# A planned attention block on one core: first rows loaded ahead of the large operands, and three small steps given a choice of two engines

## The chip, the core and the metric

The kernel runs on one core of one Trainium2 chip. The metric is the device time of one execution in microseconds (us); lower is better. The five engines are called as the profile calls them: PE (matmul; PEld is its weight load), DVE, ACT, POOL and SP. Each engine works through its own instruction stream in order, and an instruction that waits for a semaphore holds up all that stands behind it in that stream. SP only issues DMAs here.

## What is computed

The reference is a transformer block with modulation, for 2 sequences of 2048 tokens of 256 features, all in f32. Cut to what matters:

```
mod = silu(c) @ wmod                       # 6 rows of 256 per sequence: sa, ca, ga, sb, cb, gb
ga, gb = sign * max(|.|, 0.25)
h = layernorm(x) * (1 + ca) + sa
x = x + ga * attention(h)                  # 2 query heads, 1 key/value head of 128, rotary, causal
h = layernorm(x) * (1 + cb) + sb
x = x + gb * experts(h)                    # 8 experts, 256 -> 1024 -> 256, gate with a threshold
```

## The kernel before, in words

There are two stages. `experts` (from some 507 us to the end) is a loop over items of 256 tokens for each of 8 experts. Its code isn't touched. `attention` (up to some 502 us) is touched, and it isn't a loop: it is a list of small steps, each a Python function that issues a few instructions, put into an order by a planner.

**The planner.** `Plan.add` notes a step: an engine, an estimated cost in us, the steps it comes after, the buffers it takes and gives back (`room`: 6 PSUM tiles `ps`, 9 row tiles `x`, 3 `xn`, and so on), a rank, and an extra delay `late` for what a DMA takes to land. `Plan.run` plays these costs through in an event loop: whenever an engine is free, the open step with the lowest rank that is ready and finds its buffers is put on it. When all are placed, the steps are issued in the order in which they began. So the estimated costs decide the order in every engine's stream, and nothing else does; on the chip each stream then runs at its own real durations. A step can't overtake another in its stream, even when it is ready and the other isn't.

**The loads (lines 271 to 294 and 435 to 439).** `load` plans a DMA on SP at a cost of 0.06 + KB/180 us. The first ones have the rank `first` (-100) and so go in the order of the code: `c_sb` (2 KB), `wm_0` (512 KB: the weights of the first modulation), `wqkv_sb` (512 KB), the first quarter of the rotary table (512 KB). `wm_1` (1024 KB) and `wo_sb` (256 KB) have rank 0.5. A tile's own rows of x (128 KB, `load_x`) have the tile's rank.

**The modulation.** `by_feature` (L322) multiplies `wm_0` with silu(c) on PE; `by_feature_out` (L330) leaves `modT`, shift and scale by feature. For each sequence b, `gates` (L345) and `rows` (L373) are two PE steps that need `wm_1`; `gates_out` (L354 to L368, 8 instructions on DVE, scheduled as one step) makes `woG` and `gb_bc`, and `rows_out` (L380, L381) `mod_bc`. Their rank is 0.6 + 2b.

**A tile (128 tokens, `tile_steps`).** The tiles have ranks 0, 1, 2 and so on: four of sequence 0, four of sequence 1, and so on; 32 in all. The first part of a tile is what the change touches:

- load rows; mean and variance on DVE (L412, L414); 1/sqrt on POOL (L418, L419)
- `xn` (L444, DVE): rows less mean, times 1/sqrt
- `turn` (L453, PE): two transposes into PSUM, one for each half of the features
- `hT(0)` (L461, ACT) and `hT(1)` (L463, DVE): scale and shift of the two halves, PSUM to SBUF
- `qkv` (L472, PE), 128 x 512; the copy of v (L478, ACT)
- rotary: two products (L488, and L496 in two instructions), then their sum (L505), all on DVE
- `turn_rot` (L512, PE), copies of k and q (L515, L517, ACT)

Then come scores (L528, L532), row maximum (L539, L546, DVE), exponentials (L555, ACT), transposes (L601), weighted values (L611), projection (L645), residual (L652), the second layernorm (L667, L670, with 1/sqrt on POOL again), the layout copy `halves` on POOL (L677), and the gate's logits (L692, L701). After each group of tiles the gate is worked out, and POOL issues one indirect DMA for each tile into the first expert's list (L808), each after the one before it. Work of the first expert on two items (L950, L967) has rank 1000 and fills PE at the end of the stage. The loads of the first two experts' weights wait for all modulation steps, since they take the space of `wm_0`, `wm_1`, `wo_sb` and `sc_bc`.

Of the kernel before, what the change touches and what calls it, by code (L numbers as in the profile page):

```python
# [18 lines left out]
ALU = mybir.AluOpType  # L19
AX = mybir.AxisListType  # L20

P = 128
B, T, D = 2, 2048, 256
# [19 lines left out]
class Plan:  # L43
# [2 lines left out]

    def __init__(self, room):
        self.room = dict(room)  # L50
        self.steps = []

    def add(self, eng, cost, do, after=(), take=(), give=(), rank=0.0, late=0.0):


        self.steps.append((eng, cost, do, tuple(after), tuple(take), tuple(give), rank, late))
        return len(self.steps) - 1

    def run(self):
        LINK = 0.12  # L60
        need = [len(s[3]) for s in self.steps]
        then = [[] for _ in self.steps]
        for n, s in enumerate(self.steps):
            for m in s[3]:
                then[m].append(n)
        queues = {}
        ready = [0.0] * len(self.steps)
        open_ = {n for n, c in enumerate(need) if c == 0}
        free, ends, order, now = {}, [], [], 0.0
        while open_ or ends:  # L70
            for n in sorted(open_, key=lambda n: (self.steps[n][6], n)):
                eng, cost, do, _, take, give, _, late = self.steps[n]
                if free.get(eng, 0.0) > now or ready[n] > now:
                    continue
                if any(self.room[r] < take.count(r) for r in take):
                    continue
                for r in take:
                    self.room[r] -= 1
                free[eng] = now + cost
                ends.append((now + cost + late, n))  # L80
                open_.discard(n)
                order.append(n)
            times = [e for e, _ in ends] + [f for f in free.values() if f > now]
            times += [ready[n] for n in open_ if ready[n] > now]
            now = min(t for t in times if t > now)
            for e, n in [x for x in ends if x[0] <= now]:
                ends.remove((e, n))
                for r in self.steps[n][5]:
                    self.room[r] += 1
                for m in then[n]:  # L90
                    need[m] -= 1
                    ready[m] = max(ready[m], e + LINK)
                    if need[m] == 0:
                        open_.add(m)
        assert len(order) == len(self.steps)
        for n in order:
            self.steps[n][2]()
        return now


# [92 lines left out]
def attention(  # L193
# [5 lines left out]
    nc = tc.nc  # L199
# [17 lines left out]
        return small.tile(shape, dtype, tag=tag, name=f"{tag}{u}")  # L217

    plan = Plan(room)
    first = -100.0  # L220


# [13 lines left out]
    wqkv_sb = const.tile([P, KD, 4 * HS], F32, name="wqkv_sb")  # L236
# [33 lines left out]

    def load(dst, src, kb, rank=first, **how):
        return plan.add(
            "SP", 0.06 + kb / 180.0, lambda: nc.sync.dma_start(dst, src), late=2.0, rank=rank, **how
        )


    l_c = load(c_sb, cT.rearrange("(k p) b -> p k b", p=P), 2)
    l_x0 = None
    wm = wmod.rearrange("(k p) f -> p k f", p=P)
    l_m0 = load(wm_0, wm[:, :, : 2 * D], 512)  # L280
    l_qkv = load(wqkv_sb, wqkvT.rearrange("(k p) f -> p k f", p=P), 512)
    l_rope = [
        load(rope_sb[:, ds(4 * q, 4)], rope.rearrange("(q n p) (z f) -> p q n z f", p=P, n=4, z=2)[:, q],
             512, rank=first if q == 0 else q * 8 - 7.5)
# [2 lines left out]

    sheet_of_0 = lists[0].rearrange("(p c) f -> p c f", p=P)
    load(sheet_of_0[:, : AHEAD * CI, :], kept.front, 8, rank=0.7)
    l_m1 = load(wm_1, wm[:, :, 2 * D :], 1024, rank=0.5)  # L290
    l_wo = load(wo_sb, woT.rearrange("(h p) d -> p h d", p=P), 256, rank=0.5)
    l_wg = load(wgt_sb, wgt.rearrange("(k p) e -> p k e", p=P), 9, rank=0.5)
    l_bg = load(bgt_sb, bgt.partition_broadcast(P), 5, rank=0.5)
    l_b1 = load(b1_sb, b1T, 32, rank=6.0)
# [5 lines left out]
    def load_expert(e):  # L300
        w1_e = wpool.tile([P, KD, FF], F32, tag=f"w1_{e}", name=f"w1_{e}")
        nc.sync.dma_start(w1_e, w1[e].rearrange("(k p) f -> p k f", p=P))
        w2_e = wpool.tile([P, NF, D], F32, tag=f"w2_{e}", name=f"w2_{e}")
        nc.sync.dma_start(w2_e, w2[e].rearrange("(f p) d -> p f d", p=P))
        weights.append((w1_e, w2_e))
# [8 lines left out]
        after=[s_sc], rank=first,  # L314
# [24 lines left out]
    for b in range(B):  # L339

        def gates(b=b):
            box["pg", b] = pg = ps_tile(f"pg{b}")
            for g, which in enumerate((2, 5)):
                for k in range(KD):
                    nc.tensor.matmul(  # L345
                        pg[:, ts(g, D)], sc_bc[:, k, b, :], wm_1[:, k, ts(which - 2, D)],
                        start=(k == 0), stop=(k == KD - 1),
                    )

        def gates_out(b=b):  # L350

            u = f"_g{b}"
            g_sb = work([P, 2 * D], "g_sb", u)
            nc.vector.tensor_copy(g_sb, box["pg", b])  # L354
            sign = work([P, 2 * D], "sign", u)
            nc.vector.tensor_scalar(sign, g_sb, 0.0, 2.0, ALU.is_ge, ALU.mult)
            size = work([P, 2 * D], "size", u)
            nc.vector.scalar_tensor_tensor(size, g_sb, -1.0, g_sb, ALU.mult, ALU.max)
            nc.vector.tensor_scalar(size, size, 0.25, None, ALU.max)
            ga = work([P, D], "ga", u)  # L360
            nc.vector.scalar_tensor_tensor(
                ga, sign[:, :D], 1.0, size[:, :D], ALU.subtract, ALU.mult
            )
            nc.vector.scalar_tensor_tensor(
                gb_bc[:, b, :], sign[:, D:], 1.0, size[:, D:], ALU.subtract, ALU.mult
            )
            for h in range(NH):
                nc.vector.tensor_tensor(woG[:, b, h, :], wo_sb[:, h, :], ga, ALU.mult)  # L368

        def rows(b=b):  # L370
            box["pr", b] = pr = ps_tile(f"pm2{b}")
            for k in range(KD):
                nc.tensor.matmul(  # L373
                    pr, sc_bc[:, k, b, :], wm_1[:, k, D : 3 * D],
                    start=(k == 0), stop=(k == KD - 1),
                )

        def rows_out(b=b):
            pr = box["pr", b]
            nc.vector.tensor_copy(mod_bc[:, b, :D], pr[:, :D])  # L380
            nc.vector.tensor_scalar(mod_bc[:, b, D:], pr[:, D:], 1.0, None, ALU.add)  # L381

        r = 0.6 + 2 * b
        g = plan.add("PE", 1.8, gates, after=[s_bc, l_m1], take=["ps"], rank=r)
        m_wo.append(plan.add("DVE", 4.0, gates_out, after=[g, l_wo], give=["ps"], rank=r))
        g = plan.add("PE", 1.8, rows, after=[s_bc, l_m1], take=["ps"], rank=r)
        m_mod.append(plan.add("DVE", 0.9, rows_out, after=[g], give=["ps"], rank=r))

    prev, l_first = [], []
    for e in range(RES):  # L390
        prev = [
            plan.add(
                "SP", 11.0, lambda e=e: load_expert(e), after=m_wo + m_mod + [m_T] + prev, late=2.0,
                rank=8.0 + 4 * e,
            )
        ]
        l_first += prev
# [26 lines left out]
    def tile_steps(b, i, r, group, g):  # L424
# [7 lines left out]
        def add(eng, cost, do, after=(), **how):  # L432
            return plan.add(eng, cost, do, after=after, rank=r, **how)
# [2 lines left out]
            st["x"] = work([P, D], "x", u)  # L436
            nc.sync.dma_start(st["x"], x[b, ts(i, P), :])

        n_x = add("SP", 0.8, load_x, late=2.0, take=["x"])
        n_n = moments("a" + u, st, [n_x], add)  # L440

        def xn():
            st["xn"] = work([P, D], "xn", u)
            nc.vector.tensor_scalar(  # L444
                st["xn"], st["x"], st["mv"][:, 0:1], st["rstd"], ALU.subtract, ALU.mult
            )

        n_n = add("DVE", 0.42, xn, [n_n], take=["xn"])

        def turn():  # L450
            st["pt"] = ps_tile(f"pt{u}")
            for k in range(KD):
                nc.tensor.transpose(st["pt"][:, ts(k, P)], st["xn"][:, ts(k, P)], ident)  # L453

        def hT(k):
            if "hT" not in st:
                st["hT"] = work([P, KD, P], "hT", u)
            scale_k, shift_k = modT[:, KD + k, b : b + 1], modT[:, k, b : b + 1]
            src, dst = st["pt"][:, ts(k, P)], st["hT"][:, k, :]
            if k == 0:  # L460
                nc.scalar.activation(dst, src, AF.Identity, bias=shift_k, scale=scale_k)  # L461
            else:
                nc.vector.tensor_scalar(dst, src, scale_k, shift_k, ALU.mult, ALU.add)  # L463

        n_t = add("PE", 0.32, turn, [n_n], take=["ps"], give=["xn"])
        n_0 = add("ACT", 0.27, lambda: hT(0), [n_t, m_T], take=["hT"])
        n_1 = add("DVE", 0.29, lambda: hT(1), [n_t, m_T, n_0], give=["ps"])

        def qkv():
            st["pq"] = ps_tile(f"pq{u}")  # L470
# [11 lines left out]
        def rot(z):  # L482
# [18 lines left out]
        n_r0 = add("DVE", 0.6, lambda: rot(0), [n_q, l_rope[i // 4]], take=["big"])  # L501
        n_r1 = add("DVE", 0.75, lambda: rot(1), [n_q, n_v, n_r0], give=["ps"])
        n_r = add(
            "DVE", 0.55,
            lambda: nc.vector.tensor_tensor(st["t", 0], st["t", 0], st["t", 1], ALU.add),  # L505
            [n_r0, n_r1],
        )

# [916 lines left out]
```

## Time and profile before

| what | value |
|---|---|
| median of 3 runs | 1676.8 us (1675.76 to 1677.0) |
| the profiled execution | 1677.0 us, of which its span 1675.2 us |
| PE busy over the span | 1622.3 us (97%) |
| DVE / ACT / POOL busy | 677.0 (40%) / 576.4 (34%) / 855.0 us (51%) |
| mean granted clock of PE | 0.988 |

The span is what the trace covers; 1.8 us of the execution lie outside it. A share of busy time is a mean over the two stages: in the attention stage POOL is nearly idle and DVE is nearly full at first, in the experts' stage it is the other way round. Tables by stretch of time show this, and the prediction reads such a table. PE's busy time counts a slow matmul as busy, so its clock has to be looked at beside it.

### The profile page before, as it was taken

What the parts mean: (1) busy time and instruction counts of PE and PEld (TensorE: products, weight loads), DVE (VectorE), ACT (ScalarE), POOL (GpSimd) and SP (SyncE); (2) the same over time, 40 slices, a digit from 0 to 9 for tenths busy, and PEclk for the clock granted to TensorE, in tenths of its full rate; (3) what the DMA queues carried; (4) which work ended last, traced back from release to release, by engine and by line L of the source; (5) the groups of instructions that cost most, each with busy time, mean ns of one, the idle gap of its engine ahead of it and who ended that gap; (6) DMA issues with size and microseconds to landing.
All of it is one profiled execution on the core that took longest, in us unless ns stands there. A gap on an engine that the chain in (4) does not pass through costs nothing.

```text
span 1675.2 us, 26699 instructions
## 1 busy us (share of the span) xinstructions
PE 1622.3 (97%) x7666; PEld 1352.3 (81%) x7666; DVE 677.0 (40%) x2220; ACT 576.4 (34%) x1390; POOL 855.0 (51%) x991
## 2 busy tenths in 40 slices
PE   6999999999998998999999999999999999999996
PEld 3667677676787887888888888888888888888886
DVE  5987767666642222322333222222322222222322
ACT  2555555555632222222222222222222232222222
POOL 2332222021117777756775775676677477734443
PEclk9999999999998998999999999999999999999998
DMA  6211000000024334335334433533533333433332
GB/s 218 101 39 32 26 29 29 17 13 17 13 50 101 57 63 109 58 58 108 58 60 101 78 57 61 106 59 62 109 60 61 63 58 57 67 59 57 63 57 47
DMA packets 166045, 106.36 MB, mean 63 GB/s; under 512 B 111136, under 2 KB 157344, under 8 KB 165856
## 3 DMA queue, kind: packets, MB, share of 16 engines
q0 software_dynamic: 42064, 46.84, 17.8%
q1 hardware_dynamic: 116048, 46.22, 11.7%
q10 hardware_dynamic: 7872, 12.58, 2.4%
q8 instruction: 26, 0.43, 0.1%
q14 instruction: 35, 0.29, 0.1%
HBM read 50.39 MB, written 31.87 MB: 49 GB/s over the span
## 4 chain that ended last, share of the span: by engine, by line
PE 61%; DMA 3%; issue 3%; POOL 3%; POOLq 1%; DVE 0%; SPq 0%; DVEq 0%
PE h L1145 31%; PE y L1136 30%; POOL out L1288 2%; DMA xp<-xr 1%; DMA xr<-feats,at 1%; POOL list L1278 0%; POOL xr L1257 0%; DMA out<-yo,who 0%; POOLq L1038 0%; POOL out L1320 0%; POOL at L1299 0%; POOLq L1086 0%; POOLq L1299 0%; DVE yo L1235 0%; POOL to L1270 0%
## 5 line engine op out<-in xcount | busy, mean ns | idle before, releaser
L1145 PE MATMUL h<-xT,w 128*128 128x256 f32 (+1 forms) x2752 | 660.6, 373 | 16.3 <-DVE xT L1199 8.9
L1136 PE MATMUL y<-w,g 128*128 128x256 f32 x2640 | 654.3, 379 | 0.0
L1171 ACT ACTIVATE g<-h,b_sb 128x256 f32<-128x256 f32 (+1 forms) x688 | 320.4, 466 | 847.8 <-PE h L1145 845.7
L1145 PEld LDWEIGHTS h<-xT,w 128*128 128x128 f32 x2752 | 514.7, 191 | 86.6 <-DVE xT L1199 10.5
L1136 PEld LDWEIGHTS y<-w,g 128*128 128x128 f32 x2640 | 498.8, 190 | 66.3
L1288 POOL DMA_INDIRECT out<-yo,who x173 | 283.2, 1637 | 215.1 <-DVE yo L1235 163.0
L1199 DVE COPY xT<-xp 128x512 uint16<-128x512 uint16 x172 | 68.0, 437 | 630.4 <-PE h L1145 608.0
L1278 POOL DMA_INDIRECT list<-new,to x228 | 233.7, 1025 | 99.3 <-POOL new L1273 46.7
L1257 POOL DMA_INDIRECT xr<-feats,at x172 | 173.8, 1010 | 100.9 <-POOL at L1299 70.2
L611 PE MATMUL pav<-pT,v 128*128 128x256 f32 x544 | 144.0, 387 | 0.6 <-ACT pT L605 0.5
L528 PE MATMUL psc<-kT,qT 128*128 128x512 f32 (+3 forms) x320 | 142.9, 532 | 0.3 <-DVE s L539 0.2
L539 DVE TENSOR_SCALAR_CACHE_REDUCE s<-psc 128x512 f32<-128x512 f32 (+3 forms) x160 | 96.2, 605 | 68.3 <-PE psc L528 46.0
L555 ACT ACTIVATE s<-s,nmx 128x512 f32<-128x512 f32 (+3 forms) x160 | 103.9, 651 | 46.5 <-DVE nmx L546 46.2
L611 PEld LDWEIGHTS pav<-pT,v 128*128 128x128 f32 x544 | 96.1, 192 | 29.1 <-issue 19.6
L1223 DVE TENSOR_TENSOR yb<-y,b_bc 128x256 f32<-128x256 f32 x165 | 62.6, 419 | 135.9 <-PE y L1136 135.8
L418 POOL TENSOR_SCALAR rstdf<-mvf 128x1 f32<-128x1 f32 x32 | 8.3, 260 | 195.2 <-DVE mvf L414 115.4
L605 ACT COPY pT<-ptr 128x512 f32<-128x512 f32 (+1 forms) x144 | 77.2, 563 | 52.3 <-PE pav L611 30.4
L601 PE MATMUL ptr<-ident,s 128*128 128x128 f32 x544 | 76.4, 280 | 2.7 <-ACT s L555 2.7
L601 PEld LDWEIGHTS ptr<-ident,s 128*128 128x128 f32 x544 | 65.6, 145 | 16.6 <-ACT s L555 5.0
L1214 DVE SCALAR_TENSOR_TENSOR gate<-gb_bc,mcur,part 128x256 f32<-128x256 f32 x172 | 75.8, 482 | 3.0
L808 POOL DMA_INDIRECT list<-entry,place x32 | 33.7, 1054 | 76.9 <-DVE place L805 56.6
L528 PEld LDWEIGHTS psc<-kT,qT 128*128 128x128 f32 x320 | 57.5, 190 | 14.0 <-issue 6.3
(157 smaller groups left out, 1069.7 us busy)
## 6 DMA issues: line engine op xcount, KB each, us to landing
w<-in_w ACTq DMA_DIRECT2D x12, 1024.0 KB, 7.8
x<-in_x SPq DMA_DIRECT2D x32, 128.0 KB, 2.1
out<-x SPq DMA_DIRECT2D x32, 128.0 KB, 1.7
w<-in_w SPq DMA_DIRECT2D x4, 1024.0 KB, 9.1
feats<-hp SPq DMA_DIRECT2D x32, 128.0 KB, 1.7
list<-new,to POOLq DMA_INDIRECT x228
out<-yo,who POOLq DMA_INDIRECT x173
xr<-feats,at POOLq DMA_INDIRECT x172, 2.8
```

What stands on the lines that cost most here:

```text
L528: nc.tensor.matmul(ps[:, :w], st["qT"][:, h, :], kT[:, ds(c * SC, w)], start=True, stop=not last)
L539: nc.vector.tensor_scalar(s[:, :w], st["sc", h, c][:, :w], 1.0, None, ALU.mult, ALU.max, accum_out=st["mx", h][:, c : c + 1],)
L555: nc.scalar.activation(s[:, :w], s[:, :w], AF.Exp, bias=st["nmx", h], accum_out=st["den"][:, h, c : c + 1],)
L601: nc.tensor.transpose(ptr[:, j, h, :], s[:, ds((c0 + j) * P % SC, P)], ident)
L605: nc.scalar.copy(pT[:, :m], st["ptr", c0][:, :m])
L611: nc.tensor.matmul(st["pav"][:, : NH * P], v[:, c0 + j, :], st["pT", c0][:, j].rearrange("p h t -> p (h t)"), start=(c0 + j == 0), stop=(c ...
L1136: last = pe.matmul(ys[c], gs[f % 4][:, ts(c, P)], weights[e][1][:, f, :], start=(f == 0), stop=(f == NF - 1),)
L1145: last = pe.matmul(hs[f % 4][:, :w], weights[e][0][:, k, ts(f, P)], xT[:, k, :w], start=(k == 0), stop=(k == KD - 1),)
L1171: act.activation(gs[f % 4][:, :w], hs[f % 4][:, :w], AF.Gelu_apprx_tanh, bias=b1_sb[:, at : at + 1],).then_inc(sem["act"], 1)
L1257: pool.indirect_dma_start(out=xr[:, ts(c, 2 * D)], out_offset=None, in_=feats, in_offset=bass.IndirectOffsetOnAxis(ap=at[:, c : c + 1], ax ...
L1278: pool.indirect_dma_start(out=lists[e], out_offset=bass.IndirectOffsetOnAxis(ap=to[:, j : j + 1], axis=0), in_=new[:, j, :], in_offset=Non ...
L1288: pool.indirect_dma_start(out=rows, out_offset=bass.IndirectOffsetOnAxis(ap=who[:, c : c + 1], axis=0), in_=yo[:, c, :], in_offset=None, b ...
```

## The change

- `Plan.add` takes a list of engines with a cost for each. `Plan.run` places such a step on the first engine of the list that is free when the step is ready, and hands the engine to the step's function. Which engine it is, is fixed when the program is built; the chip doesn't choose.
- Three steps of each tile get such a list: `xn` (DVE 0.42 or POOL 0.65), `hT(1)` (DVE 0.41 or ACT 0.46), and the rotary sum L505 (DVE 0.58 or POOL 1.0).
- The costs of loads become max(0.5, KB/360); a tile's rows cost 0.5 instead of 0.8, an expert's weights 6.0 instead of 11.0.
- Ranks of loads: `c_sb` first, then the rows of tiles 0 and 1, then `wm_0` and `wqkv_sb`, then the first quarter of the rotary table and the rows of tiles 2 and 3, then `wm_1` and `wo_sb`.
- The rank of the steps of `gates` and `rows` becomes 1.6 + 3b instead of 0.6 + 2b.

```diff
     def add(self, eng, cost, do, after=(), take=(), give=(), rank=0.0, late=0.0):
+        if isinstance(eng, str):
+            eng, cost, do = [eng], [cost], lambda _, do=do: do()
...
-                eng, cost, do, _, take, give, _, late = self.steps[n]
-                if free.get(eng, 0.0) > now or ready[n] > now:
+                engs, costs, do, _, take, give, _, late = self.steps[n]
+                idle = [(e, c) for e, c in zip(engs, costs) if free.get(e, 0.0) <= now]
+                if not idle or ready[n] > now:
                     continue
+                eng, cost = idle[0]
...
-            "SP", 0.06 + kb / 180.0, lambda: nc.sync.dma_start(dst, src), late=2.0, rank=rank, **how
+            "SP", max(0.5, kb / 360.0), lambda: nc.sync.dma_start(dst, src), late=2.0, rank=rank,
...
-    l_c = load(c_sb, cT.rearrange("(k p) b -> p k b", p=P), 2)
+    l_c = load(c_sb, cT.rearrange("(k p) b -> p k b", p=P), 2, rank=first - 3)
-    l_m0 = load(wm_0, wm[:, :, : 2 * D], 512)
-    l_qkv = load(wqkv_sb, wqkvT.rearrange("(k p) f -> p k f", p=P), 512)
+    l_m0 = load(wm_0, wm[:, :, : 2 * D], 512, rank=first - 1)
+    l_qkv = load(wqkv_sb, wqkvT.rearrange("(k p) f -> p k f", p=P), 512, rank=first - 1)
-    l_m1 = load(wm_1, wm[:, :, 2 * D :], 1024, rank=0.5)
-    l_wo = load(wo_sb, woT.rearrange("(h p) d -> p h d", p=P), 256, rank=0.5)
+    l_m1 = load(wm_1, wm[:, :, 2 * D :], 1024, rank=first + 1)
+    l_wo = load(wo_sb, woT.rearrange("(h p) d -> p h d", p=P), 256, rank=first + 1)
...
-        r = 0.6 + 2 * b
+        r = 1.6 + 3 * b
...
-                "SP", 11.0, lambda e=e: load_expert(e), after=m_wo + m_mod + [m_T] + prev, late=2.0,
+                "SP", 6.0, lambda e=e: load_expert(e), after=m_wo + m_mod + [m_T] + prev, late=2.0,
...
-        n_x = add("SP", 0.8, load_x, late=2.0, take=["x"])
+        early = {0.0: -2, 1.0: -2, 2.0: 0, 3.0: 0}
+        n_x = plan.add(
+            "SP", 0.5, load_x, late=2.0, take=["x"], rank=first + early[r] if r in early else r
+        )
...
-        n_n = add("DVE", 0.42, xn, [n_n], take=["xn"])
+        n_n = add(["DVE", "POOL"], [0.42, 0.65], xn, [n_n], take=["xn"])
...
-            if k == 0:
+            if eng == "ACT":
                 nc.scalar.activation(dst, src, AF.Identity, bias=shift_k, scale=scale_k)
             else:
                 nc.vector.tensor_scalar(dst, src, scale_k, shift_k, ALU.mult, ALU.add)
...
-        n_1 = add("DVE", 0.29, lambda: hT(1), [n_t, m_T, n_0], give=["ps"])
+        n_1 = add(
+            ["DVE", "ACT"], [0.41, 0.46], lambda eng: hT(1, eng), [n_t, m_T, n_0], give=["ps"]
+        )
...
         n_r = add(
-            "DVE", 0.55,
-            lambda: nc.vector.tensor_tensor(st["t", 0], st["t", 0], st["t", 1], ALU.add),
+            ["DVE", "POOL"], [0.58, 1.0],
+            lambda eng: of[eng].tensor_tensor(st["t", 0], st["t", 0], st["t", 1], ALU.add),
             [n_r0, n_r1],
         )
```

`of` is the table from "DVE" and "POOL" to the engine's instruction issuer.

More of the change, by code (lines that the diff above doesn't have):

```diff
@@ L81, in run @@
                 open_.discard(n)
-                order.append(n)
+                order.append((n, eng))
             times = [e for e, _ in ends] + [f for f in free.values() if f > now]
@@ L95, in run @@
         assert len(order) == len(self.steps)
-        for n in order:
-            self.steps[n][2]()
+        for n, eng in order:
+            self.steps[n][2](eng)
         return now
@@ L219, in attention @@
     plan = Plan(room)
+    of = {"DVE": nc.vector, "POOL": nc.gpsimd}
     first = -100.0
@@ L272, in load @@
         return plan.add(
-            "SP", 0.06 + kb / 180.0, lambda: nc.sync.dma_start(dst, src), late=2.0, rank=rank, **how
-        )
-    l_c = load(c_sb, cT.rearrange("(k p) b -> p k b", p=P), 2)
-    l_x0 = None
+            "SP", max(0.5, kb / 360.0), lambda: nc.sync.dma_start(dst, src), late=2.0, rank=rank,
+            **how
+        )
+    l_c = load(c_sb, cT.rearrange("(k p) b -> p k b", p=P), 2, rank=first - 3)
     wm = wmod.rearrange("(k p) f -> p k f", p=P)
-    l_m0 = load(wm_0, wm[:, :, : 2 * D], 512)
-    l_qkv = load(wqkv_sb, wqkvT.rearrange("(k p) f -> p k f", p=P), 512)
+    l_m0 = load(wm_0, wm[:, :, : 2 * D], 512, rank=first - 1)
+    l_qkv = load(wqkv_sb, wqkvT.rearrange("(k p) f -> p k f", p=P), 512, rank=first - 1)
     l_rope = [
@@ L437, in load_x, with xn @@
             nc.sync.dma_start(st["x"], x[b, ts(i, P), :])
-        n_x = add("SP", 0.8, load_x, late=2.0, take=["x"])
+        early = {0.0: -2, 1.0: -2, 2.0: 0, 3.0: 0}
+        n_x = plan.add(
+            "SP", 0.5, load_x, late=2.0, take=["x"], rank=first + early[r] if r in early else r
+        )
         n_n = moments("a" + u, st, [n_x], add)
-        def xn():
+        def xn(eng):
             st["xn"] = work([P, D], "xn", u)
-            nc.vector.tensor_scalar(
+            of[eng].tensor_scalar(
                 st["xn"], st["x"], st["mv"][:, 0:1], st["rstd"], ALU.subtract, ALU.mult
             )
-        n_n = add("DVE", 0.42, xn, [n_n], take=["xn"])
+        n_n = add(["DVE", "POOL"], [0.42, 0.65], xn, [n_n], take=["xn"])
         def turn():
@@ L453, in turn, with hT @@
                 nc.tensor.transpose(st["pt"][:, ts(k, P)], st["xn"][:, ts(k, P)], ident)
-        def hT(k):
+        def hT(k, eng):
             if "hT" not in st:
@@ L465, in tile_steps @@
         n_t = add("PE", 0.32, turn, [n_n], take=["ps"], give=["xn"])
-        n_0 = add("ACT", 0.27, lambda: hT(0), [n_t, m_T], take=["hT"])
-        n_1 = add("DVE", 0.29, lambda: hT(1), [n_t, m_T, n_0], give=["ps"])
+        n_0 = add("ACT", 0.27, lambda: hT(0, "ACT"), [n_t, m_T], take=["hT"])
+        n_1 = add(
+            ["DVE", "ACT"], [0.41, 0.46], lambda eng: hT(1, eng), [n_t, m_T, n_0], give=["ps"]
+        )
         def qkv():
```

## The prediction, made before the changed kernel was built

> **What bounds the kernel.** The page gives PE 97% of the span, so only time in which PE is idle or slow can be won. I read the stretches of time first. Columns: stretch, length, busy time of PE, PEld, DVE, ACT and POOL with instruction counts, granted PE clock, DMA share, GB/s.
>
> ```profile
> 0.00:10.00 10.00, 3.54 (x16) 3.49 (x16) 2.67 (x7) 1.49 (x2) 3.99 (x19) 1.00 0.80 243
> 10.00:20.00 10.00, 5.57 (x13) 2.48 (x14) 2.75 (x8) 1.24 (x4) 0.82 (x2) 1.00 0.96 300
> 20.00:30.00 10.00, 9.05 (x36) 5.63 (x34) 8.48 (x28) 2.94 (x8) 1.59 (x4) 1.00 0.23 78
> 30.00:40.00 10.00, 6.54 (x18) 3.22 (x18) 8.01 (x26) 1.82 (x5) 3.05 (x7) 0.83 0.67 221
> 40.00:60.00 20.00, 19.33 (x96) 12.97 (x97) 18.26 (x74) 12.60 (x39) 4.07 (x10) 1.00 0.43 153
> 60.00:80.00 20.00, 19.05 (x96) 13.39 (x95) 17.81 (x61) 7.89 (x27) 8.30 (x18) 1.00 0.25 80
> ...
> 200.00:250.00 50.00, 50.00 (x242) 36.02 (x241) 31.23 (x113) 27.25 (x73) 10.10 (x20) 1.00 0.08 24
> ```
>
> PE is idle for 15.3 us of the first 40 (10 less each of 3.54, 5.57, 9.05, 6.54), for 5.6 us from 40 to 200, and hardly after that. From 40 to 100 DVE is 90% busy: there it is the second bound. Next, who kept PE waiting before 40 us, and how fast its matmuls ran (waits: total, times, longest; timeline: start, length):
>
> ```profile
> PE pm L322 <- DMA wm<-in_wmod: 6.0, 1, 6.0
> PE pt L453 <- DVE xn L444: 5.2, 3, 2.4
> PE pr L512 <- DVE t L505: 2.1, 1, 2.1
> ...
> 13.05 3.78 PE L472 MATMUL pq<-wqkv_sb,hT 128*128 128x512 f32 x4 [0.55 <-ACT hT L461]
> ...
> 43.50 1.88 PE L472 MATMUL pq<-wqkv_sb,hT 128*128 128x512 f32 x4
> ...
> 8.71 5.70 SPq L437 DMA_DIRECT2D x<-in_x x5
> ...
> 26.08 0.42 DVE L412 BATCH_NORM_STATS2 sta<-x 128x6 f32<-128x256 f32 x1
> ```
>
> The same four matmuls take 3.78 us at 13.05 and 1.88 at 43.50: PE is slow until it has been busy for a while. The next two such groups take 2.93 and 2.36 us. Slowness therefore costs 1.9 + 1.05 + 0.5 = 3.4 us, and the first 40 us lose 15.3 + 3.4 = **18.7 us**. Tile 1's rows are issued only after the large loads (8.71), and its statistics stand at 26.08, behind a block of modulation work on DVE: PE runs one tile alone, and waits along its chain.
>
> At the stage's end PE finishes at 499.46 and the experts begin at 506.86. That tail hangs on PE's last result, so what PE gains earlier moves everything after it. The experts' code and data are the same: 0.
>
> **Part 1, the loads.** SP issues one DMA each 0.5 us. `wm_0` moves from 1.26 to about 2.27, behind two row loads, with 256 KB ahead of it. It landed 4.6 us after issue; I let it land at 6.9 (5.9 before), **+1.0**. Rows of tiles 0 and 1, 2.1 us from issue to landing where nothing is in front, are there at 3.4 and 3.9 (tile 0 before: 2.78 + 6.3 = 9.1). `wm_1` landed at 4.06 + 9.1 = 13.2 with 3.2 MB sent up to it; now it is 3.1 MB, so it stays. DVE is through with its constants and `sc_bc` at about 5.5; statistics (0.6), POOL (0.24 + 0.58) and `xn` (0.41) put tile 0's `xn` at some 7.4, under `by_feature`. So PE does `by_feature` 6.9 to 10.45 (3.54 as before), then transposes of two tiles; `modT` (0.23), `hT(0)` and `hT(1)` (0.46 and 0.41) lead to `qkv` at 11.9 instead of 13.05. Lost so far: 6.9 waiting, 0.7 around `hT`, 1.9 for a cold first `qkv`: 9.5. The Trainium skill (TensorE: Matmul & The Clock Gate, Part 1) says the clock is released after some 3.4 us of sustained work; by that rule `by_feature` might warm PE and save the 1.9, but in the row `qkv` ran slow right after it, with 3.6 us between. I take the row.
>
> **Part 2, the order up to 40 us.** After the first `qkv`, the second tile's `qkv` (rows here long ago) is work for the 2.07 us in which PE waited for L505, and tiles 2 and 3 (rows landing at about 10) for the waits at exponentials and at `xn` (2.37). `gates` of sequence 1 at rank 4.6 instead of 2.6 puts its DVE block (8 instructions, 0.69 + 0.43 + 0.69 + 0.43 + 0.43 + 0.42 + 0.75 = 3.8 us) behind tiles 1 to 4, not ahead of their `xn`. What was lost after the first `qkv` is 18.7 - 6.0 - 2.3 - 0.5 - 1.9 = 8.0 us. The new loss there, s, lies between 0 (all covered) and 8.0 (the block of sequence 0 still stands in DVE's stream, and PE waits behind it). I take s = 3.5, a little under half: two more tiles are ready, but one DVE block remains. Gain: 18.7 - 9.5 - 3.5 = **5.7 us** (1.2 to 9.2). The loads of the experts' weights, which wait for the modulation, come some us later; they landed about 9.1 us after issues at 33 to 37, and are first read near 470, so nothing waits.
>
> **Part 3, the choice of engines.** A step leaves DVE when DVE is busy in the plan. A tile costs DVE at most `xn` 0.40, `hT(1)` 0.40 and the sum 0.55 = 1.35 us less. Of PE's idle from 40 to 200, those named for the sum are 2.2 and for `xn` 0.2 us; clearing them while part comes back as another wait gives **2 us** (range -3 to 5: five is most of the 5.6, the loss is that of rival C in a mild form). After 200 PE waits 0.2 us for the sum in all: 0 (-1 to 3). ACT is half busy (27 of 50 us) and takes `hT(1)` in the same 0.46 us as its first half: 0.
>
> Price of the sum on POOL: no row has it. Low end: `halves` moves 512 elements in 0.61, so 384 take some 0.5 us. High end: The Trainium skill (GPSIMD Engine Reference, §3.1 and §4.1) sends elementwise work to VectorE and gives 2.6 cycles of 1.2 GHz an element with two inputs, estimate 384 x 2.17 ns = 0.83, with the 0.24 of POOL's smallest row about 1.05 us against 0.55 on DVE. I take 1.0, as the two inputs make the rule nearer. By the rule alone some 20 moved sums lengthen their tiles' chains by 0.45 x 20 = 9 us, **against** the change; by the row DVE's stream was 90% full, and a sum that queues there waits as long. PE works on other tiles meanwhile, so I charge nothing. The skill's SBUF — State Buffer (SBUF: two separate sides) adds that POOL and a DVE instruction with two SBUF inputs shut each other out. L670 is such a one: of 32, the median is 0.484 and the longest 0.696, so a collision was worth at most 0.2 us here. With POOL's new 0.6 + 1.0 us a tile, 32 of them are 6 us of DVE at the very worst, and hidden after 200.
>
> **Sum.** 5.7 + 2.0 + 0 = 7.7 us. From the profiled execution, 1677.0, it leaves 1669.3; that execution lies 0.2 above the median, so 1669.1.
>
> **Rivals.** About 0.2% (3.4 us) is what can be told from no change: 1673.4 and 1680.2.
> A, the forecast, 1669.1 (1662 to 1673.4): 0.55.
> B, the start is gained and the engines' choice brings nothing, 1676.8 - 5.7 = 1671.1: 0.10. Against it stand the waits for L505.
> C, slower: POOL's stream. Its indirect DMA to the list takes 1.05 us and it waited up to 2.4 us for the one before, 17.5 us in all; a moved `xn` or sum behind it comes late, and `turn` or `turn_rot` holds up PE's whole stream. 40 moved steps at 0.5 us are 20 us: 1676.8 - 7.7 + 20 = 1689. It decides from 22 such delays on (11 us of loss against 7.7 of gain, past 1680.2). Against it: POOL is busy for 10 of 50 us, and its 64 square roots went through the same stream. 0.22.
> D, same: s = 8, PE stalls again behind DVE's modulation block, gain 1.2: 1675.6. 0.13.
>
> Faster 0.65, same 0.13, slower 0.22. The least time is a start with s = 0 and nearly all of the 7.3 us lost from 40 to 200 (5.6 idle, and 1.7 by a granted clock of 0.83 in the stretch from 120 to 130): 16 us, 1661. To leave out no more than 2 in 10 the range goes some way into C: **1661 to 1684**; the forecast's own is 1662 to 1673.4.
>
> **What would show it.** In the changed profile: first `qkv` near 11.9; PE idle from 0 to 40 near 11 us, not 15.3, most of it before 7; statistics of tiles 1 to 3 before 13 us; PE idle from 40 to 200 near 3.5 us; the experts' first matmul near 499. C would show PE waiting for POOL at L453 and L512; D a wait of PE for L444 or L505 after 17 us. Wrong outright: PE gaps after 200, where there were none, from an order that the new costs made.

## The result: 1658.1 us, and the profile after

| | before | changed |
|---|---|---|
| median of 5 runs | 1676.8 us (1675.76 to 1678.69) | 1658.1 us (1657.47 to 1661.85) |
| ratio, 95% interval | | 0.9892 (0.9879 to 0.9906): 1.1% faster |
| profiled execution / its span | 1677.0 / 1675.2 us | 1661.85 / 1660.0 us |
| experts' first matmul | 506.86 us | 490.42 us |

18.7 us were gained where 7.7 were forecast. The attention stage ends 16.4 us earlier in the profiles; where the other 2.3 us come from isn't known. The five executions of the changed kernel differ by up to 4.4 us, and the profiled one was the longest. Stretches of time of the changed kernel (columns as in the prediction), then PE's waits up to 40 us and from 40 to 200:

```profile
0.00:10.00 10.00, 3.30 (x16) 3.33 (x17) 4.02 (x10) 1.49 (x2) 5.87 (x23) 1.00 0.74 243
10.00:20.00 10.00, 9.88 (x29) 5.53 (x29) 6.57 (x19) 2.32 (x7) 3.82 (x6) 1.00 1.06 354
20.00:30.00 10.00, 9.74 (x47) 6.24 (x46) 8.01 (x33) 7.22 (x22) 4.04 (x5) 1.00 0.25 80
30.00:40.00 10.00, 10.00 (x49) 6.70 (x48) 9.05 (x32) 4.24 (x15) 7.47 (x13) 1.00 0.23 69
40.00:60.00 20.00, 19.21 (x97) 13.79 (x96) 17.84 (x60) 10.31 (x33) 10.42 (x20) 1.00 0.71 248
60.00:80.00 20.00, 20.00 (x104) 13.87 (x103) 18.60 (x76) 12.34 (x37) 10.26 (x16) 1.00 0.21 67
...
PE pm L329 <- DMA wm<-in_wmod: 6.7, 1, 6.7
...
PE pr L525 <- POOL t L518: 2.2, 2, 1.5
PE pt L464 <- POOL xn L455: 1.3, 1, 1.3
PE ph L705 <- DVE hx L683: 0.2, 1, 0.2
```

After its first operand has landed (6.7 us, forecast 6.9) PE isn't named as waiting once up to 40 us. DVE is busy for 27.7 of these 40 us (21.9 before), and POOL for 21.2 (9.5 before). The moved steps, over the stage (count, busy, mean ns):

```profile
L455 POOL TENSOR_SCALAR xn<-x,mva,rstda 128x256 f32<-128x256 f32 x23 | 29.1, 1267 | 20.1 <-PE pt L464 18.9
L518 POOL TENSOR_TENSOR t<-t,t 128x384 f32<-128x384 f32 x23 | 23.0, 999 | 33.1 <-DVE before L764 8.1 <-DVE t L509 7.4 <-DVE ge L786 7.2
L472 ACT ACTIVATE hT<-pt,modT 128x128 f32<-128x128 f32 x58 | 23.7, 459 | 19.6 <-PE pt L464 19.6
```

23 of 32 `xn`, 23 of 32 sums and 26 of 32 `hT(1)` (58 less the 32 of `hT(0)`) left DVE.

**Where the 16.4 us come from.** PE's last matmul of the stage went from 499.46 to 482.19. PE's idle time before it: 15.3 to 7.1 us up to 40, 5.6 to 3.7 from 40 to 200, 3.1 to 2.8 after, together 10.3. The rest of that time PE was busy, 475.5 us before and 468.6 now with the same matmuls: 6.9 us less by slow matmuls alone. Most of it stands in the column of the granted clock. Rows of the kernel before, then of the changed one:

```profile
120.00:130.00 10.00, 9.15 (x41) 6.96 (x42) 7.67 (x30) 4.27 (x11) 3.44 (x6) 0.83 0.09 28
450.00:460.00 10.00, 7.88 (x35) 5.90 (x34) 7.16 (x23) 5.89 (x18) 3.89 (x5) 0.87 0.05 15
460.00:470.00 10.00, 10.00 (x58) 8.98 (x57) 4.88 (x28) 4.07 (x9) 3.12 (x5) 0.96 0.27 67
...
120.00:130.00 10.00, 10.00 (x57) 7.94 (x55) 5.22 (x24) 5.86 (x18) 4.94 (x6) 1.00 0.05 14
450.00:460.00 10.00, 10.00 (x49) 8.40 (x48) 5.41 (x21) 4.64 (x9) 3.93 (x5) 1.00 0.29 70
460.00:470.00 10.00, 10.00 (x52) 8.78 (x51) 3.93 (x24) 5.65 (x11) 1.66 (x3) 1.00 0.05 16
```

The kernel before lost 1.7 us of clock three times: from 30 to 40 us (10 us at 0.83), from 120 to 130, and from 450 to 470. That is 5.1 of the 6.9 us, and the changed kernel's rows have 1.00 in these places. The slow first `qkv` doesn't show in this column: the row from 10 to 20 has 1.00 in both kernels. The tail up to the experts' first matmul grew from 7.4 to 8.2.

### The profile page after: what moved, and what is told of

Same layout as the page of the kernel before. It is cut to its first block, busy times and chain, and to the rows that moved or that the text cites. A ratio compares the mean times of both kernels' runs of the same rounds, so it can differ in the third digit from the quotient of the medians.

```text
span 1660.0 us, 26742 instructions
## 1 busy us (share of the span) xinstructions
PE 1613.9 (97%) x7666; PEld 1347.2 (81%) x7666; DVE 659.0 (40%) x2148; ACT 584.4 (35%) x1416; POOL 904.5 (54%) x1037
## 4 chain that ended last, share of the span: by engine, by line
PE 61%; DMA 3%; POOL 3%; issue 3%; POOLq 1%; DVE 0%; DVEq 0%; SPq 0%
PE h L1158 31%; PE y L1149 31%; DMA xp<-xr 2%; POOL out L1301 2%; DMA xr<-feats,at 1%; POOL list L1291 1%; POOL xr L1270 0%; DMA out<-yo,who 0%; DMA sign_p_next<-g_sb_r_next 0%; DMA g_sb_r_next<-feats,next_at 0%; POOLq L1051 0%; POOL out L1333 0%; POOL at L1312 0%; POOLq L1099 0%; POOLq L1312 0%
## 5 line engine op out<-in xcount | busy, mean ns | idle before, releaser
L614 PE MATMUL ptr<-ident,s 128*128 128x128 f32 x544 | 72.6, 274 | 2.1 <-ACT s L568 1.9
L1312 POOL COPY at<-sheet 128x2 int32 x85 | 62.9, 740 | 14.5 <-DMA xp<-xr 13.5
```

The costliest lines, as they stand in the source:

```text
L614: nc.tensor.transpose(ptr[:, j, h, :], s[:, ds((c0 + j) * P % SC, P)], ident)
```

## The experiments

The mark in all of them is the experts' first matmul. A second profile of the changed kernel (b1) had it at 489.3 instead of 490.4, so a difference of 1 us says nothing. Total times serve less: beside six of the runs (a1 to a4, e1, e2) the kernel before itself took some 1700 us, and in the profiles of these six the experts' stage is 17 to 36 us longer than in the first profile of the kernel before. Each row of the table is one profiled execution; `delay` is the planner's assumed delay between engines, otherwise 0.12 us. `idle` is PE's before its last matmul of the stage, `slow` its busy time over 468.6 us, `tail` the gap to the mark; with 468.6 us they add up to the mark.

| kernel | mark | idle to 40 / to 200 / after | slow | tail |
|---|---|---|---|---|
| before | 506.9 | 15.3 / 5.6 / 3.1 | 6.9 | 7.4 |
| d2 before, delay 0.13 | 507.9 | 14.3 / 7.0 / 2.9 | 7.0 | 8.2 |
| d4 before, delay 0.11 | 512.0 | 15.6 / 4.6 / 5.8 | 9.4 | 8.1 |
| c4 before, new step costs | 514.4 | 15.3 / 5.3 / 5.0 | 10.7 | 9.6 |
| d1 loads alone | 501.5 | 10.0 / 6.0 / 2.4 | 6.3 | 8.3 |
| a1 loads and step costs, no choice | 507.7 | 10.4 / 6.7 / 5.0 | 7.5 | 9.6 |
| e1 choice alone | 505.3 | 15.7 / 4.2 / 2.6 | 5.9 | 8.3 |
| a2 choice and step costs | 506.8 | 15.2 / 3.1 / 6.7 | 5.0 | 8.2 |
| c1 choice and load costs | 499.4 | 12.7 / 1.4 / 3.1 | 5.4 | 8.2 |
| b2 changed, old load costs | 500.8 | 12.0 / 2.3 / 4.6 | 4.8 | 8.6 |
| a3 changed, rows by rank | 490.1 | 8.5 / 1.5 / 2.1 | 1.1 | 8.3 |
| a4 changed, old modulation rank | 494.0 | 8.5 / 3.7 / 2.7 | 2.0 | 8.6 |
| b3 changed, `xn` on DVE | 490.3 | 7.6 / 1.3 / 3.4 | 0.7 | 8.7 |
| b4 changed, sum on DVE | 496.1 | 7.7 / 3.5 / 3.4 | 3.3 | 9.6 |
| c3 changed, `hT(1)` on DVE | 494.7 | 9.3 / 2.9 / 1.5 | 4.2 | 8.3 |
| c2 changed, choice for the sum only | 494.7 | 9.4 / 3.1 / 2.9 | 3.1 | 7.7 |
| changed | 490.4 | 7.1 / 3.7 / 2.8 | 0 | 8.2 |
| b1 changed again | 489.3 | 6.9 / 2.3 / 2.6 | 0.7 | 8.2 |
| d3 changed, delay 0.13 | 489.6 | 6.9 / 3.4 / 3.1 | 0.4 | 7.3 |
| e2 changed, delay 0.11 | 486.9 | 7.4 / 1.3 / 1.1 | 0.5 | 8.0 |

**One part without the other.** The theory after the result was that loads and ranks fill the start, and the choice helps later.

```diff
 a1, against the changed kernel (a2 is the kernel before with the three lists of the "-" line)
-["DVE", "POOL"], [0.42, 0.65]   ["DVE", "ACT"], [0.41, 0.46]   ["DVE", "POOL"], [0.58, 1.0]
+["DVE"], [0.42]                 ["DVE"], [0.41]                ["DVE"], [0.58]
```

> The changed kernel with all three steps on their first engine (DVE) at the new costs; loads, load costs and ranks as changed. Theory L (the loads and ranks fill the start, the choice only helps between 40 and 200 us): PE idle up to 40 us stays near 7 us, the time is 1661 to 1666, that is 3 to 8 us above the changed kernel's 1658. Theory C (the start too is filled only because DVE is relieved): PE idle up to 40 us goes back to 11 or more, time 1668 to 1675.

> The kernel before with the choice of engines only: loads, their costs and all ranks as before. Theory L: PE loses nearly as much as before up to 40 us (idle 13 to 15 us), and the gain is 2 to 5 us: 1672 to 1675. Theory C: gain of 9 us or more, 1668 or less.

Measured against the kernel before: a1 1.0019 (1.0002 to 1.0036), a2 1.001 (0.9993 to 1.0026). Neither gains: both theories fall. a1 wins 5 us up to 40 (idle 10.4 instead of 15.3) and gives them back later as waits, slow matmuls and tail; a2's idle time at the start is the old one, 15.2.

**Which loads.**

```diff
 a3:  -early = {0.0: -2, 1.0: -2, 2.0: 0, 3.0: 0}
      +early = {}
 a4:  -r = 1.6 + 3 * b
      +r = 0.6 + 2 * b
 b2:  -max(0.5, kb / 360.0)   0.5 (rows)   6.0 (an expert)
      +0.06 + kb / 180.0      0.8          11.0
 c1:  a2 with b2's "-" costs, all ranks as before
```

> The changed kernel, but the rows of tiles 0 to 3 are loaded by their tiles' ranks again, after the large operands (wm_1 and wo_sb stand ahead of them). Theory L in the form that the early rows are what fills PE: PE idle up to 40 us is 12 us or more and the time 1664 to 1668. Theory R (the planner's new costs and ranks make the better order by themselves, rows early or not): idle 8 to 10, time 1659 to 1662.

> The changed kernel with the modulation's ranks as before (0.6 + 2b). If the block of sequence 1 ahead of tiles 2 to 4 on DVE is what made PE wait at 30 us before, PE idle up to 40 us rises by 2 to 3 us and the time is 1660 to 1662. If the early rows alone cover it, the time stays within 1 us of the changed kernel (1657 to 1659).

> The changed kernel with the old estimated costs on SP (0.06 + KB/180, 0.8 for a tile's rows, 11.0 for an expert's weights); ranks, early rows and choice as changed. Theory P (the planner's knowledge of when operands land is what fills PE, as a kernel without early rows kept the whole gain): experts' first matmul at 500 or later. Theory K (ranks and choice suffice): 489 to 493.

> The kernel before with two parts of the change: the choice of engines and the new estimated costs of loads; the loads' order, the early rows and the modulation's ranks as before. Theory P (the planner must know that operands land early, and must be able to relieve DVE; the loads' real order hardly matters): experts' first matmul at 488 to 494, nearly the whole gain of 16 us. Theory L (the loads' order and ranks carry half of it): 497 or later.

> The changed kernel unaltered, as a measure of how far the end of the attention stage (the experts' first matmul) repeats from execution to execution and chip to chip: 490.4 us in the first profile. If the stage is the same within 0.5 us here, profiles can be compared by that mark even where the total time varies by 20 us through the experts' stage. If it moves by more than 2 us, the mark is no use.

By the mark, a3 keeps the whole gain (490.1): the early rows, which name the change, bring nothing to the attention stage. `wm_0` is there at 5.7 instead of 6.7, and PE does both sequences' modulation while rows come. Its total time, 0.995 (0.9925 to 0.9975) of the kernel before, shows only half of the gain, with an experts' stage of 1204 us where the first profiles have 1168 and 1170. a4 loses 3.6 us (its total: 0.993 (0.9898 to 0.9963)); its idle time at the start rose by 1.4 us, less than the 2 to 3 expected. b2 loses 10.4. The likely reason, which no run isolates, is that with the old costs the plan holds everything back until loads that it thinks slow have landed. But c1, where the costs alone join the choice, stays at 499.4, so the order doesn't hang on costs alone: ranks count as well.

**Which step.**

```diff
 b3: xn on DVE only    b4: sum on DVE only    c3: hT(1) on DVE only    c2: xn and hT(1) on DVE only
```

> The changed kernel with xn on DVE only. If every microsecond of DVE relief counts, 23 xn of 0.41 us come back to DVE (9 us) and the experts' first matmul goes from 490 to 494 or later. If the sum's relief is enough (POOL's xn took 1.24 us against 0.65 planned, so it may even hurt): 488 to 491.

> The changed kernel with the rotary sum on DVE only. 23 sums of 0.56 us come back to DVE (13 us). If DVE is what bounds the start and the stretch to 200 us: experts' first matmul at 496 or later, more than without the choice for xn. If any one of the choices is enough: 488 to 492.

> The changed kernel with hT(1) on DVE only. If relief by the sum and xn is enough: 489 to 492. If hT(1) has an effect of its own (it stands right in front of PE's qkv): 494 or later.

> The changed kernel with the choice for the rotary sum alone; xn and hT(1) on DVE. If the sum is the relief that counts: 490 to 494. If hT(1) on ACT was the other half (without any choice the stage ended at 507.7, without the sum's at 496.1): 497 or later.

`xn` on POOL brings nothing (490.3), the sum 5.7, `hT(1)` 4.3. The sum alone (c2, between its two expected ranges) leaves 4.3 to be had. All three left out (a1) cost 17.3, more than their sum. The single figures are close to the 3.5 us by which the changed kernel's own draws differ (next), so they give no more than an order.

**Luck of the order.** A changed number of the planner gives a new order of the same steps, called a draw here.

```diff
 c4, on before:  -0.29 (hT(1))  0.55 (sum)
                 +0.41          0.58
 d2, d3:         -LINK = 0.12
                 +LINK = 0.13     (d4, e2: 0.11)
```

> The kernel before with only the estimated costs of hT(1) (0.29 to 0.41) and of the sum (0.55 to 0.58) as in the change: nothing else moves, so the order alone is drawn anew. Theory O (much of the 16 us is luck of the order): the experts' first matmul moves by 4 us or more from 506.9. Otherwise it stays within 3 us of it.

> The kernel before with one number of the planner moved that means nothing for the change: the assumed delay between engines 0.13 instead of 0.12 us. It draws the order anew. Theory O (order luck is worth several us): the experts' first matmul leaves 506.9 by 3 us or more. Otherwise within 2 us.

> The kernel before with the planner's delay 0.11, a second draw of its order. Together with 506.9, the draw at 0.13 and the one by new step costs (514.4) it gives the spread that an order by itself makes: theory O says 5 us or more between the ends, otherwise 3 or less apart from the one at 514.4.

> The changed kernel with the planner's delay 0.13. Theory O: it leaves 489.9 (the mean of 490.4 and 489.3) by 3 us or more. If a plan with room on DVE is robust, it stays within 2 us, and the scatter of the kernels before is greater.

> The changed kernel with the planner's delay 0.11, a second draw of its order beside 489.6 at 0.13. If room on DVE makes every order good: 488 to 492. If the two draws so far were chance: 493 or later.

Four draws of the kernel before end at 506.9, 507.9, 512.0 and 514.4: the assumed delay moved the end by 1.0 us in d2 and by 5.1 in d4, and c4 by 7.5, so theory O holds in two of three. The worst came from c4, whose cost of `hT(1)`, 0.41, is nearer to the measured 0.40. The kernel before was the best of its draws. The changed kernel's draws end at 486.9 (earlier than expected), 489.6 and 490.4, all at least 16 us ahead of any of the kernel before, so chance alone didn't make the gain.

**The parts at the old step costs**, as a1 and a2 carried c4's:

```diff
 d1: a1 with 0.29 and 0.55 for DVE      e1: a2 with 0.29 and 0.55 for DVE
```

> The kernel before with the loads alone (order, early rows, their costs, the modulation's ranks); no choice, and the old estimated costs of hT(1) and the sum, which the kernel without choice (507.7) had at their new values. If the 5.7 us that the prediction gave the loads are right and the new step costs hid them: experts' first matmul at 498 to 502. If the loads bring nothing without the relief of DVE: 505 or later.

> The kernel before with the choice of engines alone, at the old estimated costs for DVE (hT(1) 0.29, sum 0.55); with the new ones the stage ended at 506.8. If the choice alone is worth the 2 us that the prediction gave it: 503 to 506. If the draws of before (506.9, 507.9, 512.0, 514.4) are the yardstick, the choice is worth 4 to 6 us against their mean of 510.3: 503 to 507 again, and only 500 or less would show a greater part.

Loads alone 5.4 us, the choice alone 1.6, together 16.4. By means over draws: before 510.3, loads 504.6 (d1, a1), choice 506.0 (e1, a2), both 489.1: 5.7 and 4.3 alone, 21.2 together. Some 10 us belong to neither part, more than the spread of draws; what a part brings alone is less than that spread. By the table's columns, 3.3 of the 9.4 us of d1 and e1 are idle time up to 40 (5.3 and -0.4 alone, 8.2 together) and 5.3 are slow matmuls (0.6 and 1.0 alone, 6.9 together).

**What the two do together.** PE's timeline of d1, loads alone, and under it DVE's (start, length, engine, line, op; idle before, releaser):

```profile
29.13 0.22 PE L545 MATMUL psc<-maskb,identb 128*128 128x128 bf16 x1
32.68 0.69 PE L705 MATMUL ph<-ident,hx 128*128 128x128 f32 x2 [3.33 <-DVE nmx L559]
33.16 1.12 PE L614 MATMUL ptr<-ident,s 128*128 128x128 f32 x4
34.08 3.62 PE L485 MATMUL pq<-wqkv_sb,hT 128*128 128x512 f32 x4
...
25.10 0.66 DVE L361 COPY g_sb_g<-pg 128x512 f32<-128x512 f32 x1
...
27.99 0.75 DVE L375 TENSOR_TENSOR woG<-wo_sb,ga_g 128x256 f32<-128x256 f32 x2
28.90 1.00 DVE L665 SCALAR_TENSOR_TENSOR x<-po,rd,x 128x256 f32<-128x256 f32 x2 [0.16 <-PE po L658]
```

With rows early the tiles come together, and so do their DVE steps. DVE does sequence 1's modulation from 25.1 to 28.7, PE waits 3.33 us for what stands behind it, and then runs slow: `qkv` takes 3.62 us where 1.88 is its full speed (granted clock 0.66 from 30 to 40 us). In the changed kernel this block comes only after 39 us. In a4 sequence 1's `gates` come as early (PE L352 at 20.95), but with the choice, and PE's longest wait up to 40 us after `wm_0` is 0.62. So it isn't the block's place alone. From a4's DVE and POOL:

```profile
22.88 0.69 DVE L361 COPY g_sb_g<-pg 128x512 f32<-128x512 f32 x1
...
17.73 1.00 POOL L518 TENSOR_TENSOR t<-t,t 128x384 f32<-128x384 f32 x1 [2.11 <-DVE t L509]
31.54 0.23 POOL L425 TENSOR_SCALAR rstdf<-mvf 128x1 f32<-128x1 f32 x1 [12.80 <-DVE mvf L421]
```

A sum on POOL and two `hT` on ACT (21.15) are done ahead of the block, and DVE starts it 2.2 us earlier than in d1. POOL does nothing beside it. That the room ahead of the block is what saves PE the wait is read from these two traces; no run isolates it. The other way round, e1 has the choice, but its plan still takes the rows to be late: tile 1's statistics stand at 27.20 in DVE's stream, behind sequence 0's block (before: 26.08), so POOL gets no `xn` until 29.64. PE waits 2.32 us for an `xn` from DVE and 1.56 for one from POOL.

```profile
11.55 0.69 PE L464 MATMUL pt<-ident,xn 128*128 128x128 f32 x2 [2.32 <-DVE xn L455]
...
33.41 0.44 PE L464 MATMUL pt<-ident,xn 128*128 128x128 f32 x2 [1.56 <-POOL xn L455]
```

## Why the prediction was wrong, point by point

**Bound and place: right.** PE's lost time was the thing to win; part 1's dates held: `wm_0` 6.7 (6.9), first `qkv` 11.3 (11.9), no change of the experts' code needed. But PE wasn't free of losses after 200, as the prediction had it: the kernel before was idle there for 3.1 us and lost 1.7 of clock.

**The size: wrong, 16.4 (18.7 by the medians) against 7.7.** Two steps failed. The first is the sum 5.7 + 2.0 as one of two independent parts, and in it the term **s = 3.5**, "two more tiles are ready, but one DVE block remains". Alone the parts are worth what the sum said, 5.4 and 1.6, and PE's idle time after `wm_0` is 3.5 us in d1 (10.0 less 6.5); since s was a choice between 0 and 8.0, that it fits so well is partly luck. Together, s was 0.3 (7.1 less 6.7 is all of PE's idle time after `wm_0`, 0.1 of it around `hT`): the choice of part 3, priced only from 40 to 200, also works at the start. That is 3.2 us. The waits for `wm_0` and around `hT` came out 0.8 less and the first `qkv` 0.5, so the start brought 10.2 instead of 5.7. The second and larger step: slow matmuls after 40 us, put at nothing, brought 4.9. With 1.8 and 0.3 of idle time from 40 to 200 and after it, less 0.8 of tail, that makes the 16.4.

**Slow matmuls: mis-sized.** I took 3.4 us of slowness up to 40 into the loss, let 1.9 stay, counted 1.7 at 120 to 130 for the range only, and put 0 from 200 on. In fact 6.9 us went. It isn't luck of one draw: the `slow` column has 6.9 to 10.7 for the draws of the kernel before and 0 to 0.7 for those of the changed one. Two `qkv` now take 5.07 us, where eight such matmuls take 3.70 at full speed (changed kernel, then a3):

```profile
11.32 5.07 PE L485 MATMUL pq<-wqkv_sb,hT 128*128 128x512 f32 x8
...
23.78 3.70 PE L485 MATMUL pq<-wqkv_sb,hT 128*128 128x512 f32 x8 [0.33 <-ACT hT L472]
```

So 1.4 of the 1.9 stayed, as the row had said. The rule of the Trainium skill (TensorE: Matmul & The Clock Gate, Part 1), full speed after some 3.4 us of sustained work, doesn't show here: `by_feature` and the transposes, 4.6 us of work, stand right ahead of the slow `qkv`. The measurement decides. The rest, 4.9, went after 40 us, and the losses of clock often stand behind a wait of PE. Not behind each: of two waits for the same exponential, the one of the kernel before is followed by 3.4 us at half clock, the one of the changed kernel isn't.

```profile
457.07 1.40 PE L601 MATMUL ptr<-ident,s 128*128 128x128 f32 x7 [2.12 <-ACT s L555]
457.50:460.90 3.40, 3.40 (x19) 3.40 (x17) 3.03 (x10) 3.34 (x10) 2.32 (x3) 0.50 0.03 6
...
440.75 2.73 PE L614 MATMUL ptr<-ident,s 128*128 128x128 f32 x23 [1.90 <-ACT s L568]
441.00:451.00 10.00, 9.74 (x65) 8.70 (x64) 4.46 (x20) 7.20 (x18) 3.11 (x4) 1.00 0.28 70
```

The length alone doesn't decide: in a4, 1.29 us of waiting for an `xn` from POOL were enough, and the `qkv` behind it took 3.49 us. What decides stays open.

**40 to 200:** 1.8 us of idle time against 2.0: the number is right, by luck. The named waits that were to be cleared, 2.4 us for the sum and `xn`, came back as 3.5 for the same steps on POOL; what went is some 3 us of other waits, most of them for ACT's `hT` and exponentials and for DVE's row maximum.

**Price of POOL:** the sum took 0.999 us (taken: 1.0). `xn` took 1.27, which I never priced and called 0.6; the plan said 0.65. Its choice brought nothing (b3). The exclusion of POOL and DVE (the Trainium skill, SBUF — State Buffer, SBUF: two separate sides), weighed at 0.2 us at most, is there and larger: L680 took 1.82 us once and 1.14 another time (0.476 in the median), the second of them beside a sum on POOL:

```profile
51.42 1.00 POOL L518 TENSOR_TENSOR t<-t,t 128x384 f32<-128x384 f32 x1
...
51.56 1.14 DVE L680 SCALAR_TENSOR_TENSOR hx<-x,mvf,mod_bc 128x256 f32<-128x256 f32 x1
```

L680 and L683 together grew by 2.8 us over the stage, under the 6 set as the worst.

**Rivals:** C (POOL's stream) shows as 3.5 us of waits, two of them over 1 us, not 22 delays. D fell. B's gain of 5.7 is what d1 measured as a kernel of its own, 5.4, not what the change brought. An edit that the sum left at nothing, the new estimates of two steps, moved the end later in three pairs: by 7.5 us (c4), 6.2 (a1 against d1) and 1.5 (a2 against e1). No run takes it out of the changed kernel. The range's low end of 1661 was set by 9.2 + 7.3 us of losses; slowness after 200 wasn't in it.

**Left open:** why the new step costs make the worse order, and the share of each rank; no run isolates the order of `wm_1` and `wo_sb`.

## What to carry to other kernels

Two reliefs of one pipeline needn't add up (here 5.4 and 1.6 alone, 16.4 together): operands that arrive early need room on the next engine, and room needs operands, so price them together and look for the block that stands in that engine's stream. A plan from estimated costs has luck of its own: redraw it with a meaningless change (here worth up to 5.1 us) before a small gain is credited to an edit. PE's idle time can be paid twice, once as a gap and once as slow matmuls after it (here 10.3 and 6.9 us), so read the clock beside the gaps over the whole stage.

## What the hardware showed unexpectedly

- A one-input `tensor_scalar` with two per-partition operands on 128x256 takes 1.27 us on POOL, more than a two-input add of 128x384 at 1.00 (DVE, before: 0.40 and 0.55).
- In the six runs beside which the kernel before took some 1700 us, the experts' stage was 17 to 36 us longer with the same code: in a1 PE waited 11.5 us in 13 places for ACT's `g` and 8.3 us for no named cause from 520 to 1640, waits of up to 2.4 us that the changed kernel's first profile doesn't have at all. Which resource it was stays open.
